# A scan beside attention: two fewer slots of drain between the scan and the stages that follow it

## The chip, the cores and the metric

The kernel runs on one core of a Trainium2 chip. The metric is the device time of one execution in microseconds (us). Before the change the median of three runs is 3586.82 us (3584.00 to 3589.47).

## What is computed

The reference takes 32 sequences of 256 tokens of 256 numbers. It runs a block with a selective scan over each sequence and then a transformer of two layers with local attention. Cut to what matters (`xc` after the convolution, normalised to `xn`; `h` has 16 states by 512 channels for each sequence):

```python
xr, gate = split(x @ W_in.T); xr = xr + t_emb
xn = layernorm(silu(conv4(xr)))
Bm, Cm, dt = split(xn @ W_xproj.T, 3)
Ad = 1 + tanh(dt @ W_dt.T + b_dt) * 0.01 * A
Bd = Bm * minimum(norm(xn), 1)
for t in range(256):                       # one after the other
    h = clip(h * Ad[t] + Bd[t] * xn[t], -10, 10)
    y[t] = Cm[t] . h
x = ((y + D * xn) * silu(gate)) @ W_out.T
for layer in range(2):
    q, k, v = split(shift(x) @ wqkv)       # 8 heads of 64
    q, k = rotary_xpos(l2norm(q) * qs, l2norm(k) * ksc)
    x = x + local_attention(q, k, v, window=128) @ wo
    a, g = split(layernorm(shift(x)) @ w1 + b1)
    x = x + (a * gelu(g)) @ w2 + b2
```

## The kernel before

**Groups and slots.** The 32 sequences make four groups of eight (GB). The scan runs over a group's 256 time steps, with the eight sequences and the 16 states on the 128 partitions and the 512 channels along them. One time step is one *slot*; the four groups follow each other, so slots 0 to 1023 hold steps. A *chunk* is 32 slots (CH), and a group has eight chunks.

`group_scan` (from L377) enters each piece of work in an agenda under a slot number with `at(s, what, ...)`. `scan_slots` (L933) merges the agendas of all groups, and each time it is asked it emits the work of one slot. Relative to a chunk's first slot s0, the pieces that matter here are:

- at each slot the step `h` (L716), one custom instruction on VectorE (DVE). It needs a row of `xn`, spread over the partitions, which SyncE (SP) loads with a DMA six slots ahead (`xrep`, L685) and ScalarE (ACT) scales by `beta` two slots ahead (L706)
- at slots s0+5, s0+9 and so on, `y` (L728) on TensorE (PE): the products of `h` with `Cm` for earlier steps
- from s0−38 on, convolution and normalisation of the chunk (L472, L489, L509, L548 to L593): products on GpSimd (POOL), sums `acc` on DVE
- the *figures* of the chunk: length of `xn` at s0−11 (L599), `rhs` on DVE at s0−9 (L609), the product `ps_st` on PE at s0−8 (L618), `bcd` and `beta` on DVE at s0−7 (L630 to L636), decays at s0−6 and s0−5 (L643 to L661). Counted within the chunk that is being stepped through, these are slots 21, 23, 24, 25, 26 and 27 of 32
- transposes `tz` of the gated values (L785) on PE and their product `zT` (L799) on DVE, at s0+23 and s0+25 and again 16 slots later
- the last projection (L808), a copy (L819), and `put_y` (L830), which writes the result `ys` to memory; a group's last `put_y` is at slot 272 counted from the group's begin, 16 slots after its last step.

**Stages.** Attention and feed-forward work on one sequence and one layer at a time: 4 groups x 2 layers x 8 sequences make 64 such units, called sequences below. Each has eight stages (ST, L1451). `attend`, `feed` and `fetch` (L1458 to L1500) enter the pieces under stage 8n + i:

- i = 0, 1: for the next sequence the `v` projection, then `q` and `k` (ps_qkv, L989); i = 3, 4 the same for its second half of tokens. Behind `q` and `k` follow squares on ACT (L1002), and on DVE a *rotation* of each (two products, a sum and small steps, L1005 to L1019), with POOL for the rest (L1013, L1021, L1022)
- i = 2, 3: scores (L1188, L1215), exponentials (L1227); i = 7: sums and their inverses `rinv` (L1252, L1260) and values `ov` (L1271)
- for the sequences before it: division (`oT`, L1295) at i = 4, the output product `ps_wo` (L1039) at i = 6, and the feed-forward part: normalising, `pa` (L1375) with gelu on ACT (L1386) and `ag` (L1393) on DVE in six parts from i = 4 on, the narrow product `po_f` (L1402) in two halves at i = 3 and 4, each with a sum `res` or `fo` on DVE (L1413)
- at the end of a group's second layer `load_res` (L956): SP loads the next group's scan results from `ys`.

**Who meets whom.** The main loop (L1519 to L1542) decides it. `scan_to(s)` emits slots until slot s is done. Weights are loaded between slots 100 and some 270; then `scan_to(S + DRAIN)`, the eight `load_res` of group 0, and six projections with one slot after each. From there each stage t is emitted and then a few slots. Up to stage 114 (`reload`) the slots move from where they stand to 2S + DRAIN in equal steps, about 2.19 slots a stage; after that 256 slots are spread over 128 stages, two a stage. Sixteen steady stages, which are two sequences, thus take one chunk of 32 slots, and the same stage meets the same slot in each chunk.

What each engine runs is one list, fixed when the kernel is built. The program is written in the order told above; a scheduler then arranges the instructions of each engine within what they depend on, except where the code asks to keep them in order (`keep_in_program_order`). A shift of slots against stages can therefore change the order within each list.

Of the kernel before, what the change touches and what calls it, by code (L numbers as in the profile page):

```python
# [73 lines left out]
def kernel(  # L74
# [147 lines left out]
    def program(ctx, exact):  # L222
# [736 lines left out]
        def load_weights(l, kind, i=0):  # L959
            shape, srcs = {  # L960
                "qkv": lambda: ([P, KM, DI], [wqkv[:, l, :, i * DI : (i + 1) * DI]]),
                "wo": lambda: ([P, NC_, DM], [wo[:, l]]),
                "w1": lambda: (
                    [P, KM, 2, P] if MCH[i][1] == P else [P, KM, 1, DH + MREM],
                    [w1[:, l, :, x * HID + MCH[i][0] :] for x in range(2)],
                ),
                "w2": lambda: ([P, len(MCH), DM], [w2[:, l]]),
            }[kind]()
            t = wpool.tile(shape, FP, tag=f"{kind}{i}", name=f"{kind}{i}")
            if kind == "w1":  # L970

                dst = [t[:, :, 0], t[:, :, 1]] if MCH[i][1] == P else [
                    t[:, :, 0, 0:DH], t[:, :, 0, DH:]
                ]
            else:
                dst = [t]
            for out, src in zip(dst, srcs):
                nc.sync.dma_start(out=out, in_=src[:, :, 0 : out.shape[-1]])
            wt[kind, i] = t
# [534 lines left out]
        def scan_to(s):  # L1514
            while done[0] is None or done[0] < s:
                done[0] = next(scan, 1 << 30)


        DRAIN = 18  # L1519
        for i, (kind, k) in enumerate(WEIGHTS):  # L1520
            scan_to(100 + 8 * i)
            load_weights(0, kind, k)
        scan_to(S + DRAIN)
        for b in range(GB):
# [8 lines left out]
        for t in range(max(stages) + 1):  # L1533
# [3 lines left out]
            g, r = divmod(t + 1 + group - reload, group)  # L1537
            lo, hi = (g * S + S + DRAIN), ((g + 1) * S + S + DRAIN)
            if t + 1 <= reload:
                scan_to(s0 + (2 * S + DRAIN - s0) * (t + 1) // reload)  # L1540
            else:
# [6 lines left out]
    with tc.If(fits > 0) as which:  # L1548
        with ExitStack() as es:
            program(es, False)  # L1550
    with which.Else():
        with ExitStack() as es:
            program(es, True)
# [108 lines left out]
```

## Time and profile before

| what | value |
|---|---|
| median of three runs | 3586.82 us |
| profiled execution, its own time | 3582.75 us |
| its span in the trace | 3581.0 us |
| scan alone, to the first projection of attention | 0 to 467.8 us |
| stages 0 to 113, with 2.19 slots each | about 468 to 1220 us |
| steady stages, two slots each | about 1220 to 2742 us |
| stages without scan | about 2742 us to the end, 38.85 us a sequence |
| start of ps_st (L618) in three chunks in a row | 1762.48, 1864.73, 1966.64 us |

The profile comes from one execution, whose time lies 4.07 us below the median. In lines of the timeline, the columns are start, duration, engine, line, operation, result and operands, shapes and count; a bracket at the end is the idle time of the engine just before, with what ended it. In lines of waits they are the waiting engine and line, what it waited for, total in us, times and the longest. The granted clock of TensorE was 0.992 on average.

### The profile page before, as it was taken

Reading aid. Unit: us, or ns where it says so; the run is one execution under the profiler, and the core shown is the slowest. Engines: PE = TensorE matmul, PEld = TensorE weight load, DVE = VectorE, ACT = ScalarE, POOL = GpSimd, SP = SyncE. Lnnn points to the kernel's source line nnn. Section 1 sums busy time; section 2 is a strip of 40 time slices with the busy share of each in tenths; the row PEclk is TensorE's granted clock in tenths of the full one; section 3 lists DMA queues with packets and bytes.
Section 4 is the critical chain, followed back from the end, with each engine's and each line's share of the span. In section 5 each row is a group of like instructions: output and inputs, shape, how many; then the busy total and the mean of one; then the engine's idle time right before and its main releaser. Section 6 shows DMA issues by size and latency. Waiting matters only on the chain.

```text
span 3581.0 us, 57673 instructions
## 1 busy us (share of the span) xinstructions
PE 3446.0 (96%) x20220; PEld 2253.9 (63%) x20220; DVE 2667.3 (74%) x5049; ACT 1998.7 (56%) x3599; POOL 1892.2 (53%) x1842
## 2 busy tenths in 40 slices
PE   7999989999999999999999999999999999999999
PEld 4555335666656666666666666666666677777777
DVE  5888889888788777888787778888877555555553
ACT  4666656656555665566566655655666444434442
POOL 4433477645556555655565556555544454544551
PEclk9999999999999999999999999999999999999999
DMA  7887665445354545444454555534454112011101
GB/s 207 219 221 213 198 174 149 120 117 143 109 144 125 149 141 148 130 118 127 118 142 125 138 149 140 143 106 131 114 141 122 54 50 61 13 30 38 33 27 37
DMA packets 468767, 435.68 MB, mean 122 GB/s; under 512 B 228723, under 2 KB 308084, under 8 KB 468340
## 3 DMA queue, kind: packets, MB, share of 16 engines
q1 hardware_dynamic: 384018, 419.88, 42.0%
q10 hardware_dynamic: 84450, 12.01, 2.0%
q8 instruction: 163, 2.67, 0.3%
q14 instruction: 136, 1.11, 0.1%
HBM read 383.54 MB, written 46.66 MB: 120 GB/s over the span
## 4 chain that ended last, share of the span: by engine, by line
PE 61%; DVE 19%; DMA 7%; POOL 6%; ACT 4%; issue 3%; SPq 0%; ACTq 0%; DVEq 0%; POOLq 0%
PE ps_qkv L989 13%; PE pa L1375 13%; DVE h L716 7%; PE po_f L1402 7%; DMA xrep<-xnd 5%; PE ps_wo L1039 5%; PE y L728 4%; PE ov L1271 4%; PE sc L1215 3%; PE ps_out L808 3%; PE ps_in L399 2%; PE tr_qk L1028 2%; PE rs L1252 2%; ACT xrep L706 2%; DVE acc L489 2%
## 5 line engine op out<-in xcount | busy, mean ns | idle before, releaser
L716 DVE CUSTOM_DVE_ANT_0 h<-h,xrep,lim 128x512 f32<-128x512 f32 x1024 | 961.0, 938 | 228.9 <-ACT xrep L706 196.6
L706 ACT ACTIVATE xrep<-xrep,beta 128x512 f32<-128x512 f32 x960 | 672.3, 718 | 341.4 <-DMA xrep<-xnd 219.8
L989 PE MATMUL ps_qkv<-qkv,res 128*128 128x512 f32 x1536 | 713.5, 601 | 17.9 <-DVE rinv L1260 8.4
L1375 PE MATMUL pa<-hT,w 128*128 128x256 f32 (+1 forms) x2816 | 675.1, 382 | 11.3 <-DVE zT L799 10.7
L1375 PEld LDWEIGHTS pa<-hT,w 128*128 128x128 f32 (+1 forms) x2816 | 516.9, 188 | 152.9 <-issue 35.4
L1013 POOL TENSOR_TENSOR rot<-rot,swp 128x512 f32<-128x512 f32 x256 | 339.9, 1328 | 475.3 <-DVE swp L1010 423.5
L1021 POOL TENSOR_TENSOR rn<-ss,neg_half 128x8 f32<-128x8 f32 x256 | 466.8, 1823 | 18.4 <-DVE ss L1019 7.8
L989 PEld LDWEIGHTS ps_qkv<-qkv,res 128*128 128x128 f32 x1536 | 282.2, 191 | 301.6 <-issue 241.4
L728 PE MATMUL y<-h,ly 128*32 128x512 f32 x2048 | 348.9, 609 | 16.9 <-DVE h L716 13.9
L1327 POOL TENSOR_TENSOR rstd<-ve,neg_half 128x2 f32<-128x2 f32 x64 | 46.9, 733 | 527.6 <-DVE ve L1325 511.3
L1393 DVE SCALAR_TENSOR_TENSOR ag<-pa,b_sb,ag 128x256 f32<-128x256 f32 x320 | 151.6, 474 | 222.4 <-ACT ag L1386 222.3
L1402 PE MATMUL po_f<-ag,w 128*128 128x256 f32 x1280 | 309.0, 389 | 5.9 <-DVE fo L1413 3.8
L1022 POOL TENSOR_TENSOR rot<-rot,rn 128x512 f32<-128x512 f32 x256 | 289.4, 1130 | 20.0
L1402 PEld LDWEIGHTS po_f<-ag,w 128*128 128x128 f32 x1280 | 236.8, 191 | 71.3 <-issue 12.0
L1386 ACT ACTIVATE ag<-pa,b_sb 128x256 f32<-128x256 f32 x320 | 150.2, 469 | 233.1 <-PE pa L1375 232.1
L1002 ACT ACTIVATE sq<-ps_qkv 128x512 f32<-128x512 f32 x256 | 150.8, 595 | 185.1 <-PE ps_qkv L989 119.4
L1039 PE MATMUL ps_wo<-oT,wo 128*128 128x256 f32 x1024 | 231.7, 379 | 0.5 <-DVE ag L1393 0.5
L489 DVE SCALAR_TENSOR_TENSOR acc<-xr,wc_sb,acc 128x256 f32<-128x256 f32 x384 | 195.1, 531 | 47.7 <-POOL acc L478 47.2
L1005 DVE TENSOR_TENSOR rot<-ps_qkv,rc_sb 128x512 f32<-128x512 f32 x256 | 174.8, 683 | 65.6 <-ACT sq L1002 65.0
L1039 PEld LDWEIGHTS ps_wo<-oT,wo 128*128 128x128 f32 x1024 | 194.4, 190 | 28.1 <-DVE ag L1393 0.9
L1227 ACT ACTIVATE pT<-sc 128x512 f32<-128x512 f32 x384 | 202.3, 603 | 7.6 <-PE sc L1215 5.8
L1271 PE MATMUL ov<-pT,v_sb 128*64 128x256 f32 (+1 forms) x2048 | 183.7, 330 | 19.4 <-DVE ag L1393 19.3
(160 smaller groups left out, 5482.8 us busy)
## 6 DMA issues: line engine op xcount, KB each, us to landing
xrep<-xnd SPq DMA_DIRECT2D x960, 256.0 KB
rb<-inv SPq DMA_DIRECT2D x128, 256.0 KB
xnd<-xn SPq DMA_DIRECT2D x64, 256.0 KB
qkv<-in_wqkv_dram SPq DMA_DIRECT2D x24, 512.0 KB
ahead<-xs_a SPq DMA_DIRECT2D x48, 256.0 KB
xp<-ahead SPq DMA_DIRECT2D x48, 256.0 KB
xd<-xnd SPq DMA_DIRECT2D x192, 64.0 KB
w<-in_w_dram SPq DMA_DIRECT2D x80, 128.0 KB
```

Source lines behind the costliest of these rows:

```text
L489: nc.vector.scalar_tensor_tensor(acc, xr[:, :, k : k + CH], wc_sb[:, ch, k : k + 1], acc, ALU.mult, ALU.add,)
L706: scaled = nc.scalar.activation(bx, ck[c].pop(("bx", t), bx), AF.Copy, scale=ck[c]["beta"][:, t : t + 1])
L716: nc.vector._custom_dve(TENSOR_ADD_SAT, out=h_new, in0=state["h"], in1=bx, s0=ck[c]["lim"][:, 0, t : t + 1], s1=ck[c]["lim"][:, 1, t : t + 1],
L728: nc.tensor.matmul(ck[c]["y", hb][32 * q : 32 * q + 32, :], ly[hb % 2][:, 32 * t : 32 * t + 32], ck[c].pop(("h", hb * TB + t)), start=(i = ...
L989: nc.tensor.matmul(ps, res[b][:, k, t0 : t0 + W], wt["qkv", a][:, k], start=(k == 0), stop=(k == KM - 1),)
L1013: nc.gpsimd.tensor_add(rot, rot, swp)
L1021: nc.gpsimd.tensor_tensor(rn, ss, neg_half, ALU.pow)
L1022: nc.gpsimd.tensor_mul(rot, rot, bc(rn, 2, DH))
L1039: nc.tensor.matmul(po[:, d], wt["wo", 0][:, c, d * P : (d + 1) * P], oT[:, c, :], start=(c == 0), stop=(c == NC_ - 1),)
L1271: nc.tensor.matmul(ov[r * DH : (r + 1) * DH, i, kw * W :], self.qkv[b][2][:, kw, h * DH : (h + 1) * DH], self.p.pop((b, kw, i0 + i, r)), s ...
L1375: nc.tensor.matmul(dst[x], wt["w1", m][:, k, x], self.h[:, k], start=(k == 0), stop=(k == KM - 1),)
L1402: nc.tensor.matmul(self.po[:, d], wt["w2", 0][:, m, d * P : (d + 1) * P], self.ag[m], start=(m == 0), stop=(m == len(MCH) - 1),)
```

## The change

One constant changes: the drain, the number of slots after a group's last step that are emitted before attention on that group begins.

```diff
@@ -1516,7 +1516,7 @@
                 done[0] = next(scan, 1 << 30)
 
 
-        DRAIN = 18
+        DRAIN = 16
         for i, (kind, k) in enumerate(WEIGHTS):
             scan_to(100 + 8 * i)
             load_weights(0, kind, k)
```

It is used in three places: the begin of attention (L1523, slot 272 in place of 274), the end of the first stretch (L1540), and both ends of each later stretch (L1538). So every stage from the first on is followed by slots with numbers lower by two than before; the slots of a stage, their number and the stages themselves stay. The last `put_y` of a group, at slot 272, is still emitted ahead of the `load_res` that reads what it wrote. The constant is the whole diff.

## The prediction

> **What bounds the kernel now.** I read the page's shares first, then windows by stage of the run, then the waits of PE in the steady stage, and last the PE and DVE timelines of one 32-slot chunk.
>
> ```profile
> PE 3446.0 (96%) x20220; PEld 2253.9 (63%) x20220; DVE 2667.3 (74%) x5049; ACT 1998.7 (56%) x3599; POOL 1892.2 (53%) x1842
> ```
> PE is busy for 3446.0 of 3581.0 us: 135.0 us are idle, and no reordering can win more than that.
>
> The windows (length, then busy time with the count of PE, PEld, DVE, ACT, POOL; clock; DMA share; GB/s):
> ```profile
> 0.00:468.00 468.00, 421.06 (x1777) 217.02 (x1778) 386.51 (x709) 284.68 (x523) 196.48 (x288) 0.97 0.78 213
> 468.00:1220.00 752.00, 711.79 (x4289) 449.83 (x4290) 626.04 (x1163) 447.92 (x818) 442.88 (x424) 0.98 0.48 132
> 1220.00:2742.00 1522.00, 1481.98 (x9218) 982.58 (x9216) 1215.19 (x2314) 916.79 (x1662) 875.24 (x817) 1.00 0.48 133
> 2742.00:3581.00 839.00, 831.17 (x4948) 604.51 (x4940) 439.57 (x865) 349.29 (x598) 377.64 (x313) 1.00 0.15 41
> ```
> PE's idle time is 46.9 us in the scan-only stage, 40.2 us in the first 114 attention stages, 40.0 us in the steady stage (15 chunks of about 102 us, so 2.7 us a chunk) and 7.8 us after the scan's end. The stages with both kinds of work hold 80 us of it. DVE works 83% and 80% of those stages: it is not the bound on average, but it is close enough to be late at places.
>
> Which places, by the waits of PE from 1220 to 2742 us (total, times, longest):
> ```profile
> PE ov L1271 <- DVE ag L1393: 17.8, 13, 1.4
> PE pa L1375 <- DVE zT L799: 9.0, 7, 1.9
> PE ps_qkv L989 <- DVE rinv L1260: 8.4, 14, 0.9
> ```
> These three make 35.2 of the 40.0 us: 13 to 14 times in 15 chunks, so the same wait once a chunk (the second in half of them). Sixteen stages take 32 slots, so each chunk meets the same stages in the same way; an alignment that costs 1 us costs it 15 times.
>
> **What the Trainium skill says.** "Perfetto Trace Analysis", section "Identifying the Most-Contended Engine", warns that matmul busy time is a poor measure of closeness to roofline. I use it only to find gaps: the change touches no matmul, so what can move is idle time. Its section "Optimization Strategy" says to look for gaps on that engine inside one regime, and calls a gap that repeats a consistent bubble; the 13 equal waits above are one, though here DVE's order and not a buffer makes it. "PSUM — Partial Sum Buffer", section "Engine vs sequencer instructions", says that the queues of ScalarE, VectorE and GpSimdE are strict FIFO and that matmuls start in program order. The timelines below agree: an instruction late on DVE holds what stands behind it, and a matmul that waits holds all later matmuls.
>
> **The change part by part.** DRAIN 18 to 16 adds and removes no instruction. It moves every slot from stage t to the place two slots on: a steady stage t ends at slot 2t+16 (mod 32) before, 2t+14 after.
>
> *The start.* Attention begins after slot 272, not 274. Alone, a slot takes about 1.47 us; mixed, a chunk takes 103 us against 77.7 us for two sequences of attention without a scan (2 × 38.85), so 0.79 us a slot. Two slots moved are worth 2 × (1.47 − 0.79) = 1.4 us at most. But SP issues the first res load at 463.42 us without a wait, it stands at the same position of SP's queue in the new order, and PE's first projection waits 4.33 us for it; so I take −0.7 us, between −1.4 and 0. At the end nothing is won: slots 1041 and 1042 are empty.
>
> *The 114 warm-up stages.* They still move 2.19 slots each, so slots slide past the stages by some 22 slots over the stretch; a shift by two samples nearly the same alignments. I take 0, with ±6 us from the waits that the trace shows there (1.8 to 3.2 us each, so two or three more or fewer).
>
> *The steady stage, place A: the figures of the next chunk.* Slot 23 puts rhs (L609) on DVE, slot 24 ps_st (L618) on PE. Before, they meet stage i = 4 like this, right behind the last four ps_qkv of it (1860.86 to 1864.30); first PE, then DVE:
> ```profile
> 1864.30 0.60 PE L785 MATMUL tz<-ident,xd 128*128 128x128 f32 x4
> 1864.73 0.58 PE L618 MATMUL ps_st<-rhs,sel 128*128 128x96 f32 x4
> 1865.15 1.92 PE L1375 MATMUL pa<-hT,w 128*128 128x256 f32 x8
> ```
> ```profile
> 1854.03 0.48 DVE L1413 SCALAR_TENSOR_TENSOR res<-po_f,b_sb,res 128x256 f32<-128x256 f32 x1
> ...
> 1861.37 0.88 DVE L716 CUSTOM_DVE_ANT_0 h<-h,xrep,lim 128x512 f32<-128x512 f32 x1
> 1862.18 0.42 DVE L609 TENSOR_TENSOR rhs<-tok_step,stat 128x96 f32<-128x96 f32 x2
> 1862.53 0.80 DVE L716 CUSTOM_DVE_ANT_0 h<-h,xrep,lim 128x512 f32<-128x512 f32 x1
> 1863.25 0.87 DVE L489 SCALAR_TENSOR_TENSOR acc<-xr,wc_sb,acc 128x256 f32<-128x256 f32 x2
> ...
> 1868.01 0.68 DVE L1005 TENSOR_TENSOR rot<-ps_qkv,rc_sb 128x512 f32<-128x512 f32 x1
> ...
> 1872.09 0.80 DVE L716 CUSTOM_DVE_ANT_0 h<-h,xrep,lim 128x512 f32<-128x512 f32 x1
> 1872.81 1.01 DVE L1019 TENSOR_SCALAR ss<-ss 128x8 f32<-128x8 f32 x1
> 1873.73 0.68 DVE L799 TENSOR_TENSOR zT<-tz,sg 128x512 f32<-128x512 f32 x1
> ```
> DVE makes rhs 2.1 us before ps_st starts, ahead of the two rotations of q and k (L1005 to L1019, 1868.01 to 1872.09 = 4.08 us). The new order of the queues, the same in every steady chunk, differs: on DVE the rotations come first, then h, an ss, both rhs and h; on PE the run is po_f, pa, ps_qkv (four), y, pa, tz, y, ps_st, pa, ps_wo. So rhs now stands behind 4 us of rotations, and ps_st still has pa, ps_wo and everything later behind it.
>
> Both paths start at the narrow product's first half (po_f, whose sum is L1413). DVE from L1413 to the end of rhs: 13.98 us from 1854.03 to the first rotation, less the h, rhs and h that no longer stand there (1861.37 to 1863.25 = 1.88), gives 12.10; rotations 4.08; h 0.72; ss 0.92; rhs 0.35: 18.2 us. PE from the end of that po_f to ps_st, in steps of start times from 1851.76 on: transposes, scores and the v projection 3.68, second po_f 2.69, pa 1.73, four ps_qkv 3.44, y 1.00, pa 1.73, tz 0.43, y 1.00: 15.7 us. Wait: 2.5 us. DVE may come late to L1413 (before by 2.1 us, since an h there waited 1.44 us for ACT's scaled row), and its 1.41 us of waits for POOL's products inside the 12.10 us may shrink. So A costs between 2.5 − 1.4 = 1.1 and 2.5 + 2.1 = 4.6 us a chunk; I take 2.7, as most of the lateness goes when the h counts move.
>
> *Place B: the last y of a chunk* (L728) now stands in stage i = 1 behind an h that follows both rotations. After the first of the two q, k projections PE has the second 1.72, scores 2.43 and y 0.74, 4.9 us in all; DVE has a sum 0.75, rotations 4.08 and h 0.75, 5.6 us. Wait 0.7 us; I take 0.9, from 0.6 to 1.5. Where before has this pattern, in its warm-up, it costs more:
> ```profile
> 983.54 1.05 PE L728 MATMUL y<-h,ly 128*32 128x512 f32 x2 [1.75 <-DVE h L716]
> 986.58 3.24 PE L728 MATMUL y<-h,ly 128*32 128x512 f32 x4 [1.98 <-DVE h L716]
> ```
>
> *What goes away.* The old waits come just behind the small work of slots 25 to 27 (bcd, beta, decays), which delays ag and zT on DVE. In the new order two fewer h stand ahead of beta, and the 2.7 us that PE waits at A let DVE catch up; all three waits are below 1.4 us each in the typical chunk, so I take all 2.7 us as gone. Some new small waits remain: 0.4 (0 to 1). DMAs: the loads of xrep that move along on SP's queue keep their lead of four slots over ACT's scaling, 4 × 103/32 = 13 us, against some 4.5 us to land; I take 0 for them, and a load pushed back by more than the 8 us of slack would delay its h by the rest.
>
> *Sum.* A chunk: 2.7 + 0.9 + 0.4 − 2.7 = +1.3 us; 15 chunks +19.5; start −0.7; warm-up 0: +18.8 us. Against the profiled execution (3582.75 us, of which 1.75 lie outside the span) that is 3601.5; the median of the runs shown is 4.07 us above that execution, so 3605.6 in their measure, and I say **3605 us**, +0.5%. Low end of the same mechanism: 1.1 + 0.6 + 0 − 2.7 = −1.0 a chunk; high end 4.6 + 1.5 + 1.0 − 2.7 = +4.4.
>
> **The rivals.**
> *Idle trades for idle.* PE's work is unchanged; a wait at A, taken, shortens what follows, since DVE catches up in it. The sum per chunk then ends near 0 and the time is 3584 to 3587. For it: before's own chunks range from 1.5 to 4.2 us idle at one and the same order, so waits do pass into each other. Against it: the wait at A starts a long program-order chain on PE and its size does not depend on what follows. Mechanism low ends fall here too.
> *The old waits vanish, and A and B don't come: faster.* If DVE reaches L1413 early, and POOL's products are ready, the rotations start when ps_qkv ends and not when DVE is free, and rhs is done when PE comes to ps_st. DVE then has to be 2.5 us earlier than the 12.10 us say; from that point A is 0. It is won in the 15 steady chunks: 15 × (0.9 kept at B − 2.7) = −27 us: about 3560. For it: DVE has 20% idle time in the stage. Against it: before, DVE is late at just this place.
> *Loads of res queue behind writes of ys.* The last put_y (L830) now stands directly ahead of the reloads (L956), which must read what it wrote. Before, SP waits there only 6.3 us in all; four such points of up to 4.2 us, and rows behind them late: +10 to +25 us beside the rest, about 3630.
>
> **How the numbers follow.** About 0.2%, 7 us, is what a measurement of this kernel tells from no change. Forecast (3594 to 3628, most likely 3605): 0.53. Idle for idle (3580 to 3594): 0.22. Faster (3550 to 3580): 0.20. Reloads (3625 to 3645): 0.05. So faster 0.20, same 0.22, slower 0.58. For 8 in 10 I leave out the lower half of the faster case and the reloads' upper part: 3566 to 3628. The slower case's own range is 3594 to 3628.
>
> **What would show it.** In the new profile each steady chunk should show ps_st L618 waiting about 2.7 us for DVE rhs (or the y just ahead of it for h, with the same sum), and a y L728 about 0.9 us for h; the waits of ov for ag and of pa for zT should be gone; PE's idle in the steady stage should be some 60 us, not 40; the first ps_qkv should start within 1.5 us of 467.8. If ps_st doesn't wait, the step of 12.10 us is wrong; if the old waits stay beside the new ones, the time is above 3620.

## The result: 3705 us in place of 3588

The changed kernel takes 3704.93 us in the median (four runs, 3698.63 to 3705.96), the kernel before 3588.14 us beside it (3584.0 to 3592.81): a ratio of 1.0318, with a 95% interval of 1.0303 to 1.0334. The forecast was 3605 us, slower, with a range up to 3628. The sign was right and the size was not: +117 us where +19 had been worked out.

The profiled execution after took 3698.63 us, its span is 3696.9 us. First the engines' shares, from its page:

```profile
span 3696.9 us, 57637 instructions
PE 3500.5 (95%) x20220; PEld 2281.4 (62%) x20220; DVE 2679.9 (72%) x5049; ACT 2002.1 (54%) x3599; POOL 1861.9 (50%) x1842
```

PE has the same 20220 instructions but is busy for 3500.5 us where it was 3446.0: +54.5 us for the same matmuls. Idle time is 196.4 us where it was 135.0: +61.4 us. So about half of the loss is waiting, and the other half is matmuls that take longer. The forecast had a term for the first half only. The traces also record the granted clock. The time that it takes from PE's busy time (one minus the clock, summed over the busy stretches) is 26.5 us before and 78.5 us after: 52.0 of the 54.5 us.

To see where, I take as a ruler the first feed-forward normalisation of each sequence (tp_h, L1314), which both kernels do in the same order. In the changed kernel it comes 15.1 us later for the first sequence, 14.0 us later for the thirteenth (1219.11 before, 1233.06 after), 114.2 us later for the forty-fifth and 115.9 us at the last. So nothing net is lost in the warm-up stages, and 100 us are lost in the steady stage. The first 15 us are not all the change's. PE's first 1760 matmuls and DVE's first 706 instructions come in the same order in both kernels, and at the last of them the changed kernel's profile is already 4.3 us behind: these two executions differ by that much in work that is the same. Here are the first projection and the first normalisation, before and then after:

```profile
467.82 1.20 PE L989 MATMUL ps_qkv<-qkv,res 128*128 128x512 f32 x1 [4.33 <-DMA res<-ys]
567.74 0.33 PE L1314 MATMUL tp_h<-ident,res 128*128 128x128 f32 x1
```
```profile
473.85 1.19 PE L989 MATMUL ps_qkv<-qkv,res 128*128 128x512 f32 x1 [7.25 <-DMA res<-ys]
582.89 0.33 PE L1314 MATMUL tp_h<-ident,res 128*128 128x128 f32 x1
```

From the one to the other it takes 99.9 us before and 109.0 us after; 9 us are lost there.

Twelve steady chunks, between the same normalisations (the fifteenth and the thirty-ninth), first after and then before (length, then busy time of PE, PEld, DVE, ACT and POOL, then granted clock, DMA share, GB/s):

```profile
1342.22:2660.12 1317.90, 1241.41 (x7441) 814.61 (x7440) 1000.54 (x1885) 741.78 (x1345) 696.02 (x674) 0.97 0.44 123
```
```profile
1323.23:2552.96 1229.73, 1195.41 (x7442) 793.33 (x7441) 988.70 (x1886) 739.77 (x1345) 715.64 (x674) 1.00 0.48 132
```

Divided by twelve: a chunk takes 109.83 us where it took 102.48; PE waits 6.37 us in it in place of 2.86 (+3.51), and is busy for 103.45 us in place of 99.62 (+3.83). The granted clock falls from 1.00 to 0.97, which by the same sum takes 3.1 of the 3.83 us.

The waits of PE from 1250 to 2760 us after (engine and line, what it waited for, total, times, longest):

```profile
PE y L728 <- DVE h L716: 60.5, 13, 5.2
PE po_f L1402 <- DVE res L1413: 13.4, 14, 2.0
PE po_f L1402 <- DVE fo L1413: 10.7, 13, 2.7
PE ps_st L618 <- DVE rhs L609: 0.7, 1, 0.7
```

The three old waits (ov for ag, pa for zT, ps_qkv for rinv) are gone. In their place stands one large wait a chunk, y for h, 4.65 us in the mean, and smaller ones of the narrow product po_f for DVE's sums of the sequence before, 1.9 us a chunk together. Here is the first in PE's timeline:

```profile
2145.85 0.60 PE L785 MATMUL tz<-ident,xd 128*128 128x128 f32 x4
2146.38 1.06 PE L728 MATMUL y<-h,ly 128*32 128x512 f32 x6
2152.64 1.91 PE L728 MATMUL y<-h,ly 128*32 128x512 f32 x2 [5.20 <-DVE h L716]
2154.48 1.23 PE L618 MATMUL ps_st<-rhs,sel 128*128 128x96 f32 x4
2155.51 2.85 PE L1375 MATMUL pa<-hT,w 128*128 128x256 f32 x8
```

It is place A of the prediction: tz, y, ps_st and pa in line, with y in front waiting for the h that DVE makes behind both rotations. The matmuls behind the wait are slower: eight pa take 2.85 us, at other places 1.9. The windows around it show the granted clock, in the third column from the end:

```profile
2130.00:2147.50 17.50, 17.09 (x86) 9.99 (x84) 15.43 (x30) 8.88 (x19) 12.02 (x19) 1.00 0.46 139
2147.50:2152.60 5.10, 0.00 (x0) 0.00 (x0) 5.10 (x12) 3.40 (x6) 3.38 (x4) 0.80 0.89 264
2152.60:2156.00 3.40, 3.36 (x8) 1.61 (x9) 3.40 (x6) 0.00 (x0) 3.40 (x3) 0.50 0.75 148
2156.00:2160.00 4.00, 4.00 (x17) 3.42 (x16) 3.90 (x13) 1.30 (x3) 1.72 (x3) 0.83 0.67 181
2160.00:2164.00 4.00, 4.00 (x24) 3.59 (x23) 1.97 (x4) 2.45 (x5) 2.12 (x4) 1.00 0.22 68
```

PE idles for 5.1 us while DVE has not one idle moment (5.10 of 5.10). When PE goes on, its clock is 0.50 for 3.4 us, 0.83 over the next 4 us, and full after that.

The DVE timeline of the same chunk shows how the wait got longer than worked out:

```profile
2129.07 0.81 DVE L716 CUSTOM_DVE_ANT_0 h<-h,xrep,lim 128x512 f32<-128x512 f32 x1 [1.69 <-ACT xrep L706]
...
2133.82 0.80 DVE L716 CUSTOM_DVE_ANT_0 h<-h,xrep,lim 128x512 f32<-128x512 f32 x1
2134.55 0.47 DVE L1413 SCALAR_TENSOR_TENSOR fo<-po_f,b_sb,res 128x256 f32<-128x256 f32 x1
```

PE goes on from the half of po_f that L1413 adds to its next matmul at 2130.97 us; DVE comes to L1413 at 2134.55, 3.6 us later. In front of it stands a backlog of h, sg and ss steps, behind an h that waited 1.69 us for ACT's scaled row. Counted in the same way, the lateness in the prediction's chunk of the kernel before is 2.3 us (1851.76 to 1854.03), where one h follows such a wait. In the changed kernel it is 3.6 to 3.7 us in all 13 chunks.

### The profile page after: what moved, and what is told of

The parts are those of the page before. It is cut to its first block, busy times and chain, and to the rows that moved or that the text cites. A ratio compares the mean times of both kernels' runs of the same rounds, so it can differ in the third digit from the quotient of the medians.

```text
span 3696.9 us, 57637 instructions
## 1 busy us (share of the span) xinstructions
PE 3500.5 (95%) x20220; PEld 2281.4 (62%) x20220; DVE 2679.9 (72%) x5049; ACT 2002.1 (54%) x3599; POOL 1861.9 (50%) x1842
## 4 chain that ended last, share of the span: by engine, by line
PE 59%; DVE 18%; ACT 7%; DMA 7%; POOL 5%; issue 3%; SPq 1%; ACTq 0%; DVEq 0%; POOLq 0%
PE pa L1375 13%; PE ps_qkv L989 12%; DVE h L716 7%; PE po_f L1402 6%; PE ps_wo L1039 5%; DMA xrep<-xnd 5%; PE y L728 4%; PE ov L1271 3%; ACT xrep L706 3%; PE ps_out L808 2%; DVE acc L489 2%; PE tr_qk L1028 2%; PE sc L1215 2%; PE rs L1252 2%; POOL acc L478 2%
## 5 line engine op out<-in xcount | busy, mean ns | idle before, releaser
L1375 PE MATMUL pa<-hT,w 128*128 128x256 f32 (+1 forms) x2816 | 691.1, 389 | 0.0
L1013 POOL TENSOR_TENSOR rot<-rot,swp 128x512 f32<-128x512 f32 x256 | 331.4, 1295 | 588.9 <-DVE swp L1010 534.8
L1375 PEld LDWEIGHTS pa<-hT,w 128*128 128x128 f32 (+1 forms) x2816 | 526.8, 193 | 140.5 <-issue 37.3
L1021 POOL TENSOR_TENSOR rn<-ss,neg_half 128x8 f32<-128x8 f32 x256 | 453.3, 1771 | 15.9 <-DVE ss L1019 3.6
L728 PE MATMUL y<-h,ly 128*32 128x512 f32 x2048 | 367.2, 614 | 79.1 <-DVE h L716 78.5
L1039 PEld LDWEIGHTS ps_wo<-oT,wo 128*128 128x128 f32 x1024 | 194.6, 190 | 26.5
L728 PEld LDWEIGHTS y<-h,ly 128*32 128x32 f32 x2048 | 52.7, 108 | 248.2 <-DVE h L716 126.5
```

What stands on the lines that cost most here:

```text
L728: nc.tensor.matmul(ck[c]["y", hb][32 * q : 32 * q + 32, :], ly[hb % 2][:, 32 * t : 32 * t + 32], ck[c].pop(("h", hb * TB + t)), start=(i = ...
L1013: nc.gpsimd.tensor_add(rot, rot, swp)
L1021: nc.gpsimd.tensor_tensor(rn, ss, neg_half, ALU.pow)
L1039: nc.tensor.matmul(po[:, d], wt["wo", 0][:, c, d * P : (d + 1) * P], oT[:, c, :], start=(c == 0), stop=(c == NC_ - 1),)
L1375: nc.tensor.matmul(dst[x], wt["w1", m][:, k, x], self.h[:, k], start=(k == 0), stop=(k == KM - 1),)
```

## Experiments

The runs were made on several chips, which differ (before takes 3588 to 3602 us on them), so each time is read as its distance to before on its own chip. On that measure the changed kernel is at +117 us. "A chunk" is always the mean over the twelve chunks between the normalisations above; before it is 102.48 us with 2.86 us of idle PE.

### The begin of attention and the mapping of the later stages, apart

```diff
 # begin18_rest16, in the changed kernel
-        scan_to(S + DRAIN)
+        scan_to(S + 18)
 # begin16_rest18, in the kernel before
-        scan_to(S + DRAIN)
+        scan_to(S + 16)
```

> Only the begin of attention goes back to slot 274; the mapping of all later slots to stages stays that of the changed kernel. Theory (two separate losses: about 15 us at the begin, where eight res loads stand in a row on SP ahead of rows, and about 101 us in the steady stage, where y waits some 5 us for h behind two rotations once a chunk): 3588 + 101 = about 3689 us, first feed-forward normalisation near 568 us, and the waits of y for h of 4 to 5 us once a chunk still there. Rival (the late begin is what puts the scan behind in every later chunk): about 3588 to 3600 us, no such waits.

> Only the begin of attention moves to slot 272; the mapping of all later slots to stages stays that of the kernel before. Theory of two separate losses: 3588 + 15 = about 3603 us, first feed-forward normalisation near 583 us, steady stage as before. Rival (the begin puts the scan behind everywhere): about 3700 us. A third reading, that the 15 us come from the first stages' mapping and not from the eight loads in a row: about 3588 us.

Measured: begin18_rest16 3692.29 us, +94 us (ratio 1.0249, 1.0227 to 1.0272), chunk 110.26 us, y's wait as in the changed kernel. begin16_rest18 3618.88 us, +21 us (ratio 1.006, 1.0038 to 1.0082), chunk 102.72 us. So these are two separate losses, and 94 + 21 = 115 agrees with the 117 of both within the intervals. The steady loss does not come from a scan that starts late. The first normalisation came later than expected in both, at 582.1 us in place of 568 and 591.5 in place of 583, but these executions were already 10 and 11 us late at the first projection.

### Taking rhs, or y, out of the bad place

```diff
 # figures_2_earlier, in the changed kernel
-                at(s0 - 9, figures, c)
+                at(s0 - 11, figures, c)
-                at(s0 - 8, figures_out, c)
+                at(s0 - 10, figures_out, c)
 # read_out_1_later, in the changed kernel
-                        at(s + 4 * i + 5, read_out, c, hb, i)
+                        at(s + 4 * i + 6, read_out, c, hb, i)
```

> The changed kernel, with rhs and ps_st (figures, figures_out) two slots earlier, so that rhs is made ahead of the rotations of q and k. Theory (the steady loss is rhs and h behind the rotations, with y and ps_st in line on PE): the wait of 5 us a chunk goes, granted clock back above 0.985, 3588 + 15 = about 3603 us (3590 to 3615). Rival (DVE is short of time anyway, and the wait at y is only where it shows): the wait moves to another matmul, 3680 us or more.

> The changed kernel, with every read_out (the y products) one slot later, so that y no longer stands on PE just behind the rotations' stage. Theory: as for the earlier figures, about 3603 us (3590 to 3620); if only the y wait goes and ps_st then waits for rhs instead, some 1 us less a chunk, about 3670. Rival (DVE short of time anyway): 3680 us or more.

Measured: 3718.80 us, +121 us (ratio 1.0323, 1.03 to 1.0346), and 3694.50 us, +96 us (1.0255, 1.0232 to 1.0277). Both missed my expectation, and the rival that I had named, 3680 us or more, came in both. With the y products one slot later the steady order of PE and DVE around the rotations stayed as it was, and y still waited (67.6 us, 13 times), so that run tells nothing about the place. With the figures earlier the wait of y did go, and yet the chunk took 109.49 us. The waits of PE in that run, 1250 to 2760 us:

```profile
PE po_f L1402 <- DVE res L1413: 35.4, 15, 3.2
PE po_f L1402 <- DVE fo L1413: 29.1, 13, 3.2
PE po_f L1402 <- DVE ag_rem L1393: 12.2, 11, 1.6
PE ps_qkv L989 <- DVE rinv L1260: 11.4, 13, 0.9
```

The time went from y to po_f, which waits for DVE a little earlier on the same way. My theory that rhs and h behind the rotations are the whole of it fell here. As I read it, DVE comes late to this stretch, and whoever asks DVE first pays.

### Which work makes DVE late

```diff
 # in the changed kernel, e = 2 for groups 1 to 3 (and 0 for group 0), on these lines:
 # gates_2_earlier
-                    at(s0 + s + 2, gate_th, c, ch)
+                    at(s0 + s + 2 - e, gate_th, c, ch)
...
 # all_prep_2_earlier: the gates and the lines below
 # prep_without_gates_2_earlier: these alone
-                    at(s0 - 37 + 2 * ch, conv_taps, c, ch)
+                    at(s0 - 37 + 2 * ch - e, conv_taps, c, ch)
...
-                at(s0 - 9, figures, c)
+                at(s0 - 9 - e, figures, c)
...
 # conv_norm_2_earlier: as the last, without length, figures and decays
 # before_gates_2_later: in the kernel before, e = -2 on the gates' lines
```

> The changed kernel, with the gate work of groups 1 to 3 (its projection on PE, tanh on ACT, two products on DVE) two slots earlier in the chunk, so that it meets the stages as before the change. The two runs that took rhs or y out of the bad place kept the loss of about 97 us in the steady stage, so the wait at y is a symptom. Theory: what is late is DVE (with ACT) between the rotations of i = 1 and of i = 4, because the gates moved into this stretch; then about half of the loss or more goes, 3650 us or less against 3705. Rival: the gates have no part in it, within 10 us of the changed kernel.

> The changed kernel, with all work that prepares a chunk (convolution, normalisation, figures, decays) and the gates of groups 1 to 3 two slots earlier, so that of the scan only rows, h, y and what follows y meets the stages two slots sooner. If the loss comes from the prepared work meeting the wrong stages: about 3605 to 3625 us. If it comes from h, y and their rows alone: 3690 us or more.

> The kernel before, with the gates of groups 1 to 3 two slots later, so that they alone meet the stages as after the change. If the gates make the loss: 3630 us or more. If not: within 10 us of the kernel before.

> The changed kernel with convolution, normalisation, figures and decays of groups 1 to 3 two slots earlier, the gates where the change puts them. With the gates moved too it was 3636 us, with the gates alone 3703, with the figures alone 3719. If convolution and normalisation make the gain: 3630 to 3650 us. If it takes the gates as well: 3680 us or more. A value between says that the parts act together.

> The changed kernel with convolution and normalisation of groups 1 to 3 two slots earlier, figures and decays where the change puts them, so that rhs stays behind the rotations of i = 4. Figures alone gained nothing (3719 us), both together nearly all (3623 us). If both are needed (rhs behind the rotations keeps the wait of y and ps_st alive): 3680 us or more, with y or ps_st waiting over 3 us a chunk. If convolution and normalisation are all it takes: 3640 us or less.

Measured, with the ratio to before on the same chip:

| run | us | to before | ratio (95%) | chunk, us | PE idle, us |
|---|---|---|---|---|---|
| gates_2_earlier | 3702.72 | +106 | 1.029 (1.0258 to 1.0323) | 110.07 | 6.68 |
| all_prep_2_earlier | 3635.73 | +39 | 1.0092 (1.0063 to 1.0122) | 104.96 | 4.00 |
| before_gates_2_later | 3624.82 | +29 | 1.0069 (1.0049 to 1.0089) | 104.23 | 4.38 |
| prep_without_gates_2_earlier | 3623.06 | +22 | 1.0061 (1.0044 to 1.0078) | 103.94 | 3.40 |
| conv_norm_2_earlier | 3693.71 | +97 | 1.0256 (1.0231 to 1.0282) | 108.72 | 5.44 |

The gates alone are not it: moved back alone in the changed kernel, they change nothing that is clear of noise (+106 for +117 us, the intervals overlap). Moved alone in the kernel before they cost 29 us, just under the mark of 30 at which I would have blamed them, in waits of at most 1.8 us; so they are not free either. Convolution, normalisation and figures together give back most of the steady stage: by the ruler 21 of its 100 us are still lost. That the total of +22 us equals what the begin alone costs is not the whole account, since the warm-up stages are 9 us shorter in this profile than before. Figures alone gave nothing (above), convolution and normalisation alone next to nothing. The waits of the two latter runs say how. First with convolution and normalisation alone, then with the figures as well, 1250 to 2760 us (the added line of code moves some line numbers on by one):

```profile
PE y L728 <- DVE h L716: 64.5, 13, 6.0
PE po_f L1403 <- DVE fo L1414: 4.0, 7, 1.7
PE po_f L1403 <- DVE res L1414: 3.0, 7, 0.7
PE ps_st L618 <- DVE rhs L609: 2.3, 5, 0.7
```
```profile
PE pa L1376 <- DVE beta L636: 14.4, 10, 2.4
PE po_f L1403 <- DVE res L1414: 8.9, 12, 0.9
PE po_f L1403 <- DVE fo L1414: 8.4, 10, 2.1
PE ps_qkv L990 <- DVE rinv L1261: 6.7, 10, 0.9
```

There are two bad places in one chunk. Earlier convolution shortens the waits of po_f (24.1 us to 7.0) and leaves y (60.5 to 64.5). Earlier figures remove y's wait, and po_f's grow to 76.7 us with ag_rem. With both, no wait of PE is longer than 2.4 us. I read this as a steady stage with no one culprit: the wait of 5 us is where DVE's lateness meets PE's line, and with that place open it meets PE at the next.

### Less work on DVE's way

```diff
 # less_conv_after in the changed kernel, less_conv_before in the kernel before
+                n = GB if alone else 2
                 for k in range(1, TAPS):
                     nc.vector.scalar_tensor_tensor(
-                        acc, xr[:, :, k : k + CH], wc_sb[:, ch, k : k + 1], acc,
+                        acc[:, 0:n], xr[:, 0:n, k : k + CH], wc_sb[:, ch, k : k + 1], acc[:, 0:n],
```

> The changed kernel, in which the convolution's three sums of groups 1 to 3 on DVE cover two of the eight sequences only (a part of the convolution is left out); instructions and the order on PE stay, and DVE has some 2.5 to 3 us less to do a chunk between the narrow product's first sum and the rotations of i = 4. Theory (the wait of y for h is as long as DVE's way from that sum through the rotations, and a wait over 2 us brings a slow clock on top): the wait of 5 us falls to 2 to 3 us, and with the clock a chunk falls by 3 to 5 us, 40 to 65 us in all, to about 3640 to 3665 us. Rival (PE waits for something else, and DVE's way only ends at the same time): less than 15 us.

> The same cut of the convolution's sums in the kernel before. Theory: there the rotations are not what PE waits for, so DVE's relief is worth little, 0 to 15 us. Rival (DVE's load bounds the steady stage of both kernels): as much as in the changed kernel.

Measured: 3670.46 us, +69 us (ratio 1.0199, 1.0182 to 1.0217), so 48 us less than the changed kernel's +117; and 3569.24 us, −32 us (0.9906, 0.989 to 0.9923). Both kernels leave out the sums of six of the eight sequences, 2.9 and 2.8 us of DVE time a chunk. In the changed kernel y's wait falls from 60.5 to 32.5 us, 2.5 us each, as expected, and the chunk from 109.83 to 107.52 us: PE idle 6.37 to 4.72, PE busy 103.45 to 102.81. The line of that wait, 1250 to 2760 us:

```profile
PE y L729 <- DVE h L717: 32.5, 13, 3.9
```

The clock's share falls with it, from 3.1 to 2.3 us a chunk. In the kernel before the chunk falls by 0.9 us only, 102.48 to 101.55, while the run as a whole gains more than the 15 us that I allowed: by the ruler 15.1 us lie in the steady stage and 8.9 in the warm-up stages. So DVE's way through the stretch does set y's wait, by 2.15 us for 2.9 us of DVE time, and a chunk gains 2.3 us in the changed kernel and 0.9 in the kernel before, so DVE's load does not bound both alike; but the theory that DVE's relief is worth nothing in the kernel before was too strong.

### Filling the wait

```diff
-                for ch in range(NC_):
+                for ch in list(range(NC_)) * n:
                     nc.tensor.transpose(
...
-                    at(s + 23, out_turn, c)
+                    at(s + 23, out_turn, c, 1 if alone or hb else 9)
```

> The changed kernel, with the transposes tz of the first half of each chunk of groups 1 to 3 done nine times into the same place, about 3.5 us more PE work a chunk just ahead of ps_st, where PE idles 4 to 5 us a chunk. Theory (after an idle time of 4 to 5 us the granted clock halves for a few us, which is most of the 54 us that PE's busy time grew): the clock stays near 1.0 in the steady stage, and though PE has some 45 us more to do the time falls by 25 to 45 us below the changed kernel. Rival (the clock is not set by the idle time): PE's added work only fills the wait, within 10 us of the changed kernel; if the wait was not idle by need, up to 45 us slower.

Measured: 3760.52 us, +164 us (ratio 1.0441, 1.0411 to 1.0471), 47 us more than the changed kernel; the added transposes are 24 chunks by 8 × 0.43 us = 83 us. Inconclusive on the clock: the order changed with it, ps_st now waited for rhs up to 3.9 us behind the filling and po_f up to 3.2 us, and the clock fell as before (0.975 over the run). The added work came on top of the waiting and did not fill it: PE's idle time is 6.03 us a chunk, 6.37 in the changed kernel. Why DVE came later along with PE stays open.

### The shift by itself

```diff
 # drain_17, drain_20: in the kernel before
-        DRAIN = 18
+        DRAIN = 17        # and 20
 # before_prep_1_earlier: in the kernel before, convolution to decays with e = 1
```

> The kernel before with a drain of 20 in place of 18, so all slots meet their stages two later. In its order rhs stands ahead of the narrow product's sums, and ps_st right behind the v projection, away from the rotations of i = 4. Theory (what counts is where the rotations fall among rhs, h and y): no wait over 2 us in the steady stage, within 15 us of the kernel before. Rival (fewer slots of drain are worse and more are better, since work has more time): clearly faster than before, by 20 us or more. Third: another bad alignment, over 3640 us.

> Half of the change: a drain of 17. In its order rhs and the last y of the half chunk stand ahead of the rotations of i = 4, as before the change. If what counts is this order: steady stage within 25 us of the kernel before, no wait over 2 us, about 3600 to 3630 us on a chip where before takes 3598. If the loss grows with the slots of drain taken away: about half of it, 3650 us.

> The kernel before with convolution, normalisation, figures and decays of groups 1 to 3 one slot earlier, rhs still ahead of the rotations. If the waits of the kernel before (ov and pa for DVE, 2.7 us a chunk) come from the figures' small work on DVE being late: 5 to 30 us faster than before. If DVE's load is only moved: within 10 us.

Measured: drain_20 3682.50 us, +81 us (1.0232, 1.0209 to 1.0254); drain_17 3652.30 us, +53 us (1.0153, 1.0136 to 1.017); before_prep_1_earlier 3636.52 us, +37 us (1.01, 1.0083 to 1.0117). My theory failed in all three. For drain_20 the third possibility came, another bad alignment. A larger drain is no better, so the loss is not for want of lead. For drain_17 the number is what a loss in proportion to the slots taken away would give, about 3650 us; but its long wait is another one than that of drain 16, and drain 20 loses too, so a rule of proportion does not describe it. And my reading of the order was too narrow: with drain 17 rhs is ahead of the rotations as before the change, yet another wait stands in each chunk. Waits of drain_17 and then drain_20, 1250 to 2760 us:

```profile
PE ps_qkv L989 <- ACT oT L1278: 32.2, 14, 3.0
PE ov L1271 <- DVE ag L1393: 12.7, 9, 1.5
```
```profile
PE ps_st L618 <- DVE rhs L609: 44.4, 13, 3.4
PE tr_qk L1028 <- DVE ag L1393: 13.8, 11, 2.6
```

Among 16, 17, 18 and 20, drain 18 is the only one whose waits in the steady stage all stay below 2 us.

### The begin

```diff
 # begin16_loads_apart on begin16_rest18, begin18_loads_apart on the kernel before
-        for b in range(GB):
-            load_res(0, b)
+        load_res(0, 0)
         for w in range(NW):
             for a in (2, 0, 1):
                 ats[0].project(0, w, a)
+                load_res(0, 3 * w + (2, 0, 1).index(a) + 1)
                 scan_to(done[0] + 1)
+        load_res(0, 7)
 # prep_earlier_begin18: prep_without_gates_2_earlier with scan_to(S + 18) at the begin
```

> As the run with only the begin of attention at slot 272 (3619 us, 20 us above the kernel before on its chip), but the eight res loads no longer in a row on SP: one ahead of the six projections, one after each, one at the end. If the row of eight loads, which pushes the scan's rows back on SP, makes the 20 us: within 8 us of the kernel before. If the earlier begin itself does: 15 to 25 us above it.

> The kernel before with the same spread of the res loads. There two rows already stand behind the first load, so the spread is worth little: within 8 us of the kernel before. If loads in a row hurt there too: 5 to 15 us faster.

> The changed mapping with convolution, normalisation, figures and decays of groups 1 to 3 two slots earlier (3623 us with the begin at slot 272), and the begin of attention back at slot 274. If the begin's loss of 20 us and the steady loss are separate and add: about 3603 us, level with the kernel before on its chip, perhaps the best version with the changed mapping. If they do not add: 3615 us or more.

Measured: begin16_loads_apart 3620.50 us, +21 us (1.0073, 1.0049 to 1.0096); begin18_loads_apart 3602.91 us, +4 us (1.0005, 0.9995 to 1.0015); prep_earlier_begin18 3602.44 us, +6 us (1.0012, 0.9999 to 1.0026). The eight loads in a row are not what costs; the begin two slots earlier costs 21 us with or without them. From the first projection to the first normalisation it takes 100 to 104 us with the begin at 274 (before, begin18_rest16, begin18_loads_apart) and 109 to 113 us with 272 (the changed kernel, begin16_rest18, begin16_loads_apart). With the begin alone moved, another 8 to 11 us are lost in the warm-up stages, which the changed kernel does not lose. Which wait there is the first cause stays open. In the last run the begin at 274 takes +22 to +6 us, which fits two losses that add, within the intervals. But it is level with the kernel before by another balance: by the ruler 21 us are still lost in the steady stage, and the warm-up stages are 13.5 us shorter. No version with the scan two slots earlier was faster than the kernel before.

## Why the prediction was wrong, by its steps

- *The start* was taken as −0.7 us, with the first projection within 1.5 us of 467.8. It came at 473.85, and the first normalisation 15.1 us late, of which 4.3 us stood there before the order differs at all. Moved alone, the begin costs 21 us. The step read only the first load and the first projection, and took the rest of the begin as unchanged.
- *The warm-up stages*, 0 with ±6: right in size (15.1 us late at their begin, 14.0 at their end). The argument that a shift by two samples nearly the same alignments does not hold in general: with the begin alone moved, the same stages lost 8 to 11 us.
- *Place A*: the mechanism was right, in the right place and once a chunk, with y in front of ps_st as the one that waits. The size was off: 4.65 us in the mean where 2.7 was taken and 4.6 was the upper bound. The term that was mis-sized is DVE's lateness at L1413: bounded by 2.1 us from the kernel before, and taken as nearly nothing "as most of the lateness goes"; in the new order it measures 3.6 us in every chunk. DVE's way from the start of L1413 to the end of h was worked out as 16.9 us; it took 16.7 to 17.0 us in six of the 13 chunks and 18.0 in the seven in which L1413 writes fo. PE came to that y after 15.4 us, worked out as 14.7, and stopped within it at 16.5. In the chunk shown, 3.6 + 18.0 − 16.5 = 5.1 of the 5.2 us seen.
- *Place B*, 0.9 us for the last y of a chunk: there is no such wait; y waits 13 times, all at A.
- *What goes away*, 2.7 us: right in size, all three waits are gone; whether for the reason given, no run tells. *New small waits*, 0.4 us (0 to 1): po_f for res and fo, 24.1 us in 13 chunks, 1.9 a chunk. The step did not follow DVE's lateness to the next place where PE asks for it.
- *The sum*: +1.3 us of idle PE a chunk; measured +3.5. That lies within the −1.0 to +4.4 worked out for a chunk, but the top of the stated range, 3628 us, allows only about +2.8 a chunk: the range was cut shorter than the working.
- *The missing term*: +3.83 us a chunk of slower matmuls. The sum priced a wait at its length, though page and windows have a column for the granted clock, and the kernel before showed 0.97 and 0.98 in its first two stages. The filled wait, meant to take this term away by itself, failed, so that the clock makes this term rests on the sum above (3.1 of the 3.83 us), and that the waits slow the clock on the pattern of all runs given below.
- *The rivals*: PE's idle time was not traded for idle time, and the faster case, that A would not come, was wrong on its one condition: DVE came later to L1413, not earlier. The reloads behind writes of ys did wait more (15.9 us on SP in three waits, 6.3 before), but the ruler shows no jump at them. A rival that was not on the list won: the mechanism forecast, at nearly twice the size, with a slower clock behind each of its waits.

## What to carry to other kernels

Where one engine is busy nearly all the time and another some 80%, a shift of two schedules against each other need not trade small waits for small waits: the present meeting can be the one shift in which no wait is long, and every other one tried here (16, 17 and 20 slots) lost 53 to 117 us. Price a new wait from the lateness of the engine waited for in the new order, with the backlog in front of the first common point counted, and not from its lateness in the old one; then follow that lateness to the next place. And price a wait of TensorE by its length plus what the clock loses after it.

## What was not expected of the hardware

The granted clock fell after long waits of PE and hardly after short ones, with a steep step near 2 us. For the 20 profiles of this study I took every wait of PE of 0.3 us and more between the fourteenth and the forty-fifth normalisation (those within 10 us after another of 1.5 us or more left out), and the mean granted clock in the 6 us after it:

| wait of PE, us | waits | of these with a clock below 0.9 in the next 6 us | mean clock | lost in 6 us, us |
|---|---|---|---|---|
| 0.3 to 1 | 415 | 7 | 0.995 | 0.03 |
| 1 to 1.5 | 151 | 6 | 0.989 | 0.07 |
| 1.5 to 2 | 55 | 7 | 0.964 | 0.2 |
| 2 to 2.5 | 42 | 31 | 0.787 | 1.3 |
| 2.5 to 3.5 | 60 | 55 | 0.712 | 1.7 |
| 3.5 and more | 67 | 67 | 0.568 | 2.6 |

Many of these waits are the same few places of the chunk over and over, and no run changed the length of a wait and nothing else, so this is a pattern and not an experiment. By it, a wait of 1.4 us costs about 1.4 us, one of 2.7 us some 4.4, and one of 5 us some 7.6. It fits with this that the kernel before, with the same wait 13 times but never over 2 us, keeps a clock of 1.00 in its steady stage. The traces' own record of the clock between these normalisations has 172 slow stretches in the 20 profiles, each at 0.50, of 3.4 us (100 of them), 6.8 us (71) or 10.2 us (1). All but six come with a wait of 1.5 us or more, and begin 1.6 us or more after it began; the six come with two shorter waits close together, which add up to 1.9 to 2.2 us. So it is not strictly the single wait that counts.

"TensorE: Matmul & The Clock Gate" of the Trainium skill, section "What's actually happening", describes a clock that halves after an idle window of about 3.4 us and recovers after a busy one. The halved clock and the stretches of 3.4 us or its multiples agree with that; but in these runs most waits of 2 to 3.4 us, shorter than that window, were already followed by a slow clock: 73 of 89.
